# Projecting queries and keys of two batches at once, routing in six steps, and moved weight preparation in a two-layer decoder with routed experts

## The chip, the cores and the metric

The kernel runs on one core of one Trainium2 chip. The metric is the device time of one execution in microseconds (us). Three runs of the kernel before took 1874.07, 1877.6 and 1878.22 us, so the median is 1877.6 us. All data is 32-bit float.

The core has a matrix engine (TensorE, PE in the profile, with its weight loads as PEld), a vector engine (DVE), an activation engine (ACT), a general engine (GpSimd, POOL) and a queue that issues transfers (SyncE, SP). Each engine works through its own instructions in the order of the program. Matrix results go to PSUM, which this kernel divides into 4 banks for scores and a ring of 4 more for everything else.

## The reference, cut to what matters

There are 32 batches (B) of 100 rows (S) with 256 features (D), and a context of 361 rows (SK) per batch. Attention has 16 heads of 16 features. Two post-norm decoder layers follow each other:

```python
x = layernorm(x + self_attention_0(x))              # has its own inner residual; q, k, v with bias
x = layernorm(x + cross_attention_0(x, ctx, dist))  # adds -log(dist) to the scores
x = layernorm(x + ffn_0(x))        # layernorm, clip(xn * 128 / gamma), weights rounded to -1, 0, 1
x = layernorm(x + self_attention_1(x))              # one 16x16 q, k, v weight for all heads
x = layernorm(x + cross_attention_1(x, ctx))
x = layernorm(x + moe(x))          # logits = x @ Wg + bg; the best of 8 experts, weighted by its probability
```

`gamma` is the largest absolute value of `xn` over all batches, so layer 1 can begin only when the attention of layer 0 has ended for all of them. The rounding of the feed-forward weights needs `beta`, the mean absolute weight. The last step sends each row through one expert with two 256x256 layers.

## The kernel before, in words

**Slots.** The attention of both layers is written as a list of slots. `plan_batch` (L343 to L489) puts closures at a slot number and a place from 0 to 3, and `run_slots` emits them in that order; there is no planner that weighs costs. A batch begins at `start = LAYER[l] + 5 * b`, and its self-attention at `early`, which for all but the first four batches is 18 slots ahead of it. Per slot, `run_slots` emits the scores of the step two slots ahead, the transposes and exponentials of the next step, and the sums of the present one:

```python
ahead, nxt, now = (steps.get(s + d) for d in (2, 1, 0))
centre = ahead.scores() if ahead else []
for do in centre[:2]:
    do()
side(0)
for do in centre[2:]:
    do()
for i in range(3):
    if nxt:
        nxt.turn(i)
    side(i + 1)
if now:
    now.sums()
```

A batch has one self step (16 heads at once) and four cross steps of four heads each, so five slots hold one self and four cross steps, each of another batch.

**A cross step.** PE computes scores (`sc_x`, L225). DVE adds the bias and finds the maximum in one custom instruction per head (L308), POOL subtracts the maximum (L312), PE transposes the result (L322), ACT takes the exponential (L323), PE sums over the context with the values (L332), ACT copies the sums (L334). A self step does maximum and subtraction of all heads on DVE (L266, L269), then transposes (L279), exponential (L280), sums (L286). The four score banks have one buffer: the scores of a slot wait until DVE has read those of the slot before.

**Around the steps.** Rows are transposed to features by PE with a copy on ACT (`transpose_rows`, L194 and L197). `project` makes queries or keys of one batch: four matmuls with 100 columns, each of which shows as two records, in one bank (L207); layer 1's self weight is a 128x128 diagonal block and needs two matmuls (L204). `mask_queries` scales the queries for heads of even and odd number (DVE L217, or ACT L215 where there is no bias). Keys of the context (L420, L422) and values (L433, copies L436 and L439) take two and three chunks per batch; the first two value chunks share a bank. The sums are turned and normalised (L235, L237, L239), transposed again, and multiplied by the output weight (L251); DVE adds the residual (L252), takes statistics (L73, L75), POOL turns the variance into a scale (L77, L78), and DVE writes the rows back to `x_all` (L82).

**Layer 0's end.** The feed-forward input `xn` (L444, L445) and its maximum (L446) are made per batch. `scale_of_all` reduces the maximum over partitions on POOL (L642). Layer 1 then clips `xn` (L373, L374), multiplies by the rounded weights (L380) and adds the residual (L382) ahead of its self-attention.

**Weights.** `round_weights` (L632 to L638, slot 14 place 3) takes the sum of absolute weights on DVE, reduces it over partitions on POOL (L633), and makes the rounded weights on DVE. `fold_value_bias("l1x")` (L163, L166, L167, slot 18) and `fold_heads` (L651, L655, slot 22) prepare layer 1's weights: PE matmuls whose result goes into a bias row or over the weights.

**Routing.** `router` (L454, L455) makes the logits of a batch at `start + 10`, place 1. At the last batch of a group of four (batches 28 to 30 are a group of three, 31 is alone), `probabilities` (`start + 10`, place 3: 12 DVE instructions around one exponential on ACT) and `places` (`start + 11`, place 3) follow: DVE counts the rows of the batches before (`ahead`, L553 and L554, two instructions a batch), PE adds them up (`r_p`, L557: one matmul that reads `hot`, one that reads `ahead`), DVE makes the row numbers (L559 to L561). `send` (`start + 12` on) scatters the rows to their expert's region. When all are sent, `block_table` and the expert stage follow.

## Time and profile before

| | us |
|---|---|
| median of three runs | 1877.6 |
| profiled execution | 1869.26 |
| its span, which the profile shows | 1867.5 |
| PE busy in it | 1745.7 |
| stretch 420 to 680, layer 0 in steady state: PE busy | 260.00 of 260 |
| stretch 880 to 990, the passage between the layers: PE busy | 93.43 of 110 |
| stretch 1124 to 1229.7, four batches of layer 1: PE busy | 102.09 of 105.7 |
| stretch 1760 to 1867, mostly the experts: PE busy | 72.40 of 107 |

The profile comes from one execution, 8.3 us below the median of the runs shown. Its times are counted from the start of the span. "Busy" is the time in which an engine had an instruction in work; matmuls overlap in the pipeline, so the last of a group shows a longer duration than it costs. The granted clock is the clock of PE, where 1.00 is full speed. The chain that ended last is followed back from the last instruction to what released it, so its lines give what a group cost on the path. A wait is put down to the instruction that ended last before it.

### The profile page before, as it was taken

The page shows a single profiled execution, that of the slowest core. Times are in us where ns is not written, and L with a number is a line of the kernel's source. Part 1 is how long each engine was busy: PE and PEld are TensorE (multiplying, and loading weights), DVE is VectorE, ACT ScalarE, POOL GpSimd, SP SyncE. Part 2 cuts the span into 40 slices and gives each one's busy share as a digit, 9 for nine tenths or more (in the row PEclk, how much of TensorE's full clock was granted, in tenths as well). Part 3 has the DMA queues.
Part 4 walks back from the last instruction along what each step waited for, and adds up shares of the span by engine and source line. Part 5 has one row for each costly group of instructions (what it writes and reads, how often), then busy time and mean ns, then how long its engine had stood idle before and what let it go on. Part 6 is the DMA issues. An engine that isn't in the chain of part 4 may idle for free.

```text
span 1867.5 us, 53553 instructions
## 1 busy us (share of the span) xinstructions
PE 1745.7 (93%) x21368; PEld 1334.3 (71%) x21368; DVE 1313.3 (70%) x3973; ACT 918.1 (49%) x2285; POOL 1115.9 (60%) x1687
## 2 busy tenths in 40 slices
PE   6998999999999999998799999999999999999595
PEld 5776777777777777765567777777777777776484
DVE  4665667767677676777687777777777777766576
ACT  2553555555555555554345545454545545454242
POOL 1464566666666665665166576666657666655467
PEclk9998999999999999999999999999999999999798
DMA  3200222222222322200000000000000000000094
GB/s 98 65 24 20 59 64 77 79 79 60 63 76 79 79 61 62 72 27 18 17 2 18 18 27 10 27 18 22 16 16 27 18 27 10 27 18 18 32 364 160
DMA packets 62038, 95.75 MB, mean 51 GB/s; under 512 B 7675, under 2 KB 45821, under 8 KB 61662
## 3 DMA queue, kind: packets, MB, share of 16 engines
q1 hardware_dynamic: 56190, 84.68, 15.3%
q0 software_dynamic: 3584, 6.59, 1.1%
q8 instruction: 169, 2.77, 0.6%
q10 hardware_dynamic: 2016, 1.06, 0.2%
q14 instruction: 79, 0.65, 0.1%
HBM read 58.38 MB, written 34.84 MB: 50 GB/s over the span
## 4 chain that ended last, share of the span: by engine, by line
PE 83%; DVE 8%; POOL 3%; issue 3%; ACT 1%; DMA 1%; SPq 0%; POOLq 0%; DVEq 0%; ACTq 0%
PE r_t_x L322 14%; PE sc_x L225 11%; PE r_v L433 9%; PE r_a_x L332 8%; PE r_k L420 7%; PE r_q L207 5%; PE r_t_s L279 4%; PE r_o_x L251 3%; PE sc_s L225 3%; PE r_o_s L251 3%; PE r_a_s L286 3%; PE r_n_s L235 2%; PE r_k L207 2%; DVE pr L308 2%; POOL out_dram L565 2%
## 5 line engine op out<-in xcount | busy, mean ns | idle before, releaser
L312 POOL TENSOR_TENSOR pr<-pr,mx_x 100x361 f32<-100x361 f32 x992 | 761.1, 796 | 517.0 <-DVE mx_x L308 508.3
L323 ACT ACTIVATE pT_x<-r_t_x 120x400 f32<-120x400 f32 (+1 forms) x768 | 373.8, 504 | 317.9 <-PE r_t_x L322 310.8
L322 PEld LDWEIGHTS r_t_x<-ident,pr 100*120 100x120 f32 (+1 forms) x3072 | 318.1, 140 | 111.5 <-issue 45.5
L322 PE MATMUL r_t_x<-ident,pr 100*120 100x100 f32 (+1 forms) x3072 | 386.2, 253 | 9.8 <-POOL pr L312 9.4
L308 DVE CUSTOM_DVE_ANT_0 pr<-sc_x,dist 100x361 f32<-100x361 f32 x512 | 246.5, 530 | 144.9 <-PE sc_x L225 132.2
L308 DVE CUSTOM_DVE_ANT_0 pr<-sc_x,zero 100x361 f32<-100x361 f32 x512 | 244.3, 529 | 132.5 <-PE sc_x L225 129.9
L225 PE MATMUL sc_x<-kT_x,qz_x 32*100 32x361 f32 x2048 | 224.4, 508 | 10.4 <-DVE pr_s L269 8.1
L332 PE MATMUL r_a_x<-pT_x,v_cross 120*32 120x100 f32 (+1 forms) x6144 | 186.5, 254 | 8.0 <-ACT kT_x L422 8.0
L332 PEld LDWEIGHTS r_a_x<-pT_x,v_cross 120*32 120x32 f32 (+1 forms) x6144 | 129.6, 110 | 40.9 <-ACT kT_x L422 13.0
L280 ACT ACTIVATE pT_s<-r_t_s 100x400 f32<-100x400 f32 x256 | 121.2, 503 | 67.7 <-PE r_t_s L279 67.4
L266 DVE TENSOR_REDUCE mx_s<-sc_s 100x16 f32<-100x1600 f32 x64 | 116.5, 1820 | 37.3 <-PE sc_s L225 37.3
L279 PE MATMUL r_t_s<-ident,pr_s 100*100 100x100 f32 x1024 | 120.4, 250 | 5.1 <-DVE pr_s L269 2.3
L269 DVE TENSOR_TENSOR pr_s<-sc_s,mx_s 100x1600 f32<-100x1600 f32 x64 | 116.8, 1824 | 2.2
L279 PEld LDWEIGHTS r_t_s<-ident,pr_s 100*100 100x100 f32 x1024 | 100.5, 130 | 20.0 <-issue 7.8
L225 PEld LDWEIGHTS sc_x<-kT_x,qz_x 32*100 32x100 f32 x2048 | 68.7, 161 | 51.3 <-issue 20.1
L433 PE MATMUL r_v<-c_l1x_wv,ctx 128*120 128x256 f32 (+1 forms) x384 | 102.0, 390 | 0.0
L433 PE MATMUL r_v<-c_l0x_wv,ctx 128*120 128x256 f32 (+1 forms) x384 | 100.4, 384 | 0.0
L334 ACT COPY avs_x<-r_a_x 128x100 f32<-128x100 f32 x256 | 61.4, 240 | 59.9 <-PE r_a_x L332 52.1
L420 PE MATMUL r_k<-ctx,c_l1x_wk 128*128 128x361 f32 x256 | 90.3, 476 | 0.0
L420 PE MATMUL r_k<-ctx,c_l0x_wk 128*128 128x361 f32 x256 | 90.1, 474 | 0.0
L217 DVE SCALAR_TENSOR_TENSOR qz_x<-r_q,qm_x_scale,qm_x_bias 128x200 f32<-128x200 f32 x128 | 48.4, 419 | 54.0 <-PE r_q L207 52.1
L308 DVE DVE_READ_ACCUMULATOR2_ANT mx_x<- 100x1 f32 x1024 | 84.0, 82 | 0.0
(217 smaller groups left out, 2947.4 us busy)
## 6 DMA issues: line engine op xcount, KB each, us to landing
regions<-no_token SPq DMA_DIRECT2D x23, 1161.0 KB
ctx<-in_ctxT_dram SPq DMA_DIRECT2D x64, 361.0 KB
wb<-in_experts_dram SPq DMA_DIRECT2D x32, 513.0 KB
dist<-in_dist_dram SPq DMA_DIRECT2D x32, 141.0 KB
xb<-regions SPq DMA_DIRECT2D x32, 129.0 KB
x_all<-in_x_dram SPq DMA_DIRECT2D x32, 100.0 KB
b<-in_b_dram SPq DMA_DIRECT2D x1, 1024.0 KB
regions<-x_all,place POOLq DMA_INDIRECT x32, 2.9
```

The source lines that it names most:

```text
L207: nc.tensor.matmul(ps[:, m, :], lhsT=w[:, k, m * P:(m + 1) * P], rhs=srcT[:, k, :], start=(k == 0), stop=(k == NC2 - 1))
L225: nc.tensor.matmul(dst, lhsT=qz[rows, p, k, :], rhs=kT[rows, k, :], start=True, stop=True)
L269: nc.vector.tensor_tensor(pr, sg, mx.unsqueeze(3).to_broadcast([S, NG, NG, S]), ALU.subtract)
L279: nc.tensor.transpose(pt[:, j, :], t["pr_s"][:, j, g, :], ident[:S, :S])
L280: nc.scalar.activation(t["pT_s"][:, g], pt, AF.Exp)
L308: nc.vector.tensor_tensor_reduce(pr[:, j, :SK], sc[:, j, :], bias, 1.0, LOWEST, ALU.add, ALU.max, mx)
L312: nc.gpsimd.tensor_tensor(pr[:, j, :SK], pr[:, j, :SK], mx.to_broadcast([S, SK]), ALU.subtract)
L322: nc.tensor.transpose(pt[:n, j, :], t["pr_x", g][:, j, k0:k0 + n], ident[:S, :S])
L323: nc.scalar.activation(t["pT_x", g][:n, i], pt[:n], AF.Exp)
L332: nc.tensor.matmul(av[32 * j:32 * j + 32, :], lhsT=t["v_x"][:n, i, head(g, j), :], rhs=t["pT_x", g][:n, i, j, :], start=(i == 0), stop=(i ...
L420: nc.tensor.matmul(ps, lhsT=c[sx + "_wk"][:, k, m * P:(m + 1) * P], rhs=t["ctx"][:, k, :], start=(k == 0), stop=(k == NC2 - 1))
L433: nc.tensor.matmul(ps, lhsT=t["ctx"][:, k, k0:k0 + n], rhs=c[sx + "_wv"][:, k, :], start=(k == 0), stop=(k == NC2 - 1))
```

## The change

- `plan_pair` is new. It takes the transposes, queries and keys of self-attention, the cross queries and the feed-forward of layer 0's end out of `plan_batch` and plans them for two batches at a time. `project` now has 200 columns per matmul, `mask_queries` 400 elements, the clip 400. The tiles of a pair have one buffer (`w1`), but for the masked cross queries, which have two.
- For the first four batches `early` is two slots sooner; a pair's cross queries are made nine slots ahead of its first batch (four ahead for the first pair) instead of four slots ahead of each.
- Each value chunk has a bank and a copy of its own, and the chunks stand in slots `kv + 2`, `kv + 3` and `kv + 4`.
- The router moves one slot later. `probabilities` and `places` are cut into six steps, from `start + 11`, place 3, on, alternating between places 3 and 1. The rows are sent three slots later.
- The rounding is cut: mean at slot 14, rounding at slot 18. The two folds move to slot `SLOTS * B + 3`, in the passage between the layers. Layer 1 begins three slots later.

In the program order of the changed kernel, PE has 288 matmuls fewer, DVE 96 masks and 32 clips fewer, ACT 32 key copies and 32 masks fewer and 64 value copies more; POOL has the same instructions. In the odd batches of layer 1 the first feed-forward of a pair stands in the slot of the self scores, ahead of the normalising of the cross sums on DVE. In the slot of `ahead` and `r_p` the next pair's rows are turned and its self queries projected. `L167` of the fold stands on DVE between the statistics of the last batch and the writing of its rows.

```diff
-LAYER = (0, SLOTS * B + 20)
+LAYER = (0, SLOTS * B + 23)
...
-        def project(ps, w, srcT):
+        def project(w, srcT, tag):
+            ps = bank(tag)[:, :NC2 * 2 * S].rearrange("p (m b s) -> p m b s", m=NC2, b=2)
...
-                    nc.tensor.matmul(ps[:, m, :], lhsT=w[:, k, m * P:(m + 1) * P], rhs=srcT[:, k, :],
+                    nc.tensor.matmul(ps[:, m], lhsT=w[:, k, m * P:(m + 1) * P], rhs=srcT[:, k],
                                      start=(k == 0), stop=(k == NC2 - 1))
...
+        def plan_pair(l, b):
+            first = starts(l, b)
...
+            def turned(key, kind, i):
+                if i == 0:
+                    u[key] = w1.tile([P, NC2, 2, S], F32, tag=f"xT_{kind}", name=f"xT_{kind}{tag}")
+                transpose_rows(xs[b + i], kind, f"{l}_{b + i}", dst=u[key][:, :, i, :])
...
+            early = first[1]
...
+            if l:
+                at(early - 8, 2, clipped)
+                for i in range(2):
+                    at(early - 7 + i, 1, lambda i=i: feed_forward(i))
+                    at(early - 6 + i, 1, lambda i=i: centre_and_scale(xs[b + i], both[i]["y_f"], both[i]["ln_f"]))
+            for i in range(2):
+                at(early - 4, 0, lambda i=i: turned("xT", "s", i))
+            at(early - 4, 2, self_queries)
+            if l == 0:
+                at(early - 3, 1, self_keys)
+            cross = first[0] - (9 if b else 4)
+            for i in range(2):
+                at(cross, 0, lambda i=i: turned("x2T", "x", i))
+            at(cross, 2, cross_queries)
+
+        def starts(l, b):
+            return LAYER[l] + SLOTS * b, LAYER[l] + (2 * b - 10 if b < 4 else SLOTS * (b - 4) + 2)
...
-                at(early - 7, 2, keep("xq", clipped))
-                at(early - 6, 1, keep("ln_f", feed_forward))
-                at(early - 5, 1, lambda: centre_and_scale(xs[b], t["y_f"], t["ln_f"]))
-            at(early - 4, 0, keep("xT", lambda: transpose_rows(xs[b], "s", tag)))
-            at(early - 3, 0, self_queries)
-            if l == 0:
-                at(early - 3, 1, self_keys)
...
-            at(start - 4, 0, keep("x2T", lambda: transpose_rows(xs[b], "x", tag)))
-            at(start - 4, 2, keep("qz_x", cross_queries))
...
-            at(kv + 2, 3, lambda: cross_values(1))
-            at(kv + 3, 1, lambda: cross_values(2))
+            at(kv + 3, 1, lambda: cross_values(1))
+            at(kv + 4, 1, lambda: cross_values(2))
...
-                at(start + 10, 1, router)
+                at(start + 11, 1, router)
...
-                    at(start + 10, 3, lambda: probabilities(first, n))
-                    at(start + 11, 3, lambda: places(first, n))
+                    for i, do in enumerate((centred_logits, exponentials, one_hot, ahead_of, counted, rows_of)):
+                        at(start + 11 + (i + 1) // 2, 3 if i % 2 == 0 else 1, lambda do=do: do(first, n))
...
-        at(14, 3, round_weights)
-        at(18, 3, lambda: fold_value_bias("l1x"))
-        at(22, 3, fold_heads)
+        at(14, 3, mean_weight)
+        at(18, 3, rounded_weights)
+        at(SLOTS * B + 3, 0, lambda: fold_value_bias("l1x"))
+        at(SLOTS * B + 3, 0, fold_heads)
```

## The prediction, made before the changed kernel ran

> **What bounds the kernel now.** I read the page first: the busy shares, the slices with the granted clock, the chain that ended last, by engine.

> ```profile
> span 1867.5 us, 53553 instructions
> PE 1745.7 (93%) x21368; PEld 1334.3 (71%) x21368; DVE 1313.3 (70%) x3973; ACT 918.1 (49%) x2285; POOL 1115.9 (60%) x1687
> PE 83%; DVE 8%; POOL 3%; issue 3%; ACT 1%; DMA 1%; SPq 0%; POOLq 0%; DVEq 0%; ACTq 0%
> ```

> TensorE (PE) carries the end; the DVE and POOL shares say where something else does. The busy time by stretch shows where that is (us, then busy us of PE, PEld, DVE, ACT, POOL, granted clock, DMA).

> ```profile
> 150.30:158.00 7.70, 0.00 (x0) 0.00 (x0) 5.30 (x8) 0.24 (x1) 0.40 (x1) 0.68 0.00 0
> 420.00:680.00 260.00, 260.00 (x3309) 200.46 (x3308) 186.75 (x551) 142.70 (x352) 164.00 (x242) 1.00 0.27 71
> 897.00:912.00 15.00, 9.92 (x69) 7.31 (x67) 7.04 (x14) 3.73 (x10) 1.65 (x4) 0.89 0.09 25
> 1043.60:1068.80 25.20, 24.89 (x323) 18.92 (x322) 18.54 (x56) 13.32 (x34) 15.80 (x25) 1.00 0.05 17
> 1068.80:1098.80 30.00, 27.30 (x328) 20.70 (x327) 21.58 (x77) 13.37 (x35) 17.92 (x28) 0.94 0.07 21
> 1077.60:1079.80 2.20, 0.05 (x2) 0.01 (x1) 1.96 (x11) 0.46 (x1) 1.60 (x4) 1.00 0.00 0
> 1079.80:1085.50 5.70, 5.70 (x50) 4.25 (x51) 3.84 (x16) 1.25 (x3) 3.10 (x5) 0.70 0.00 0
> ```

> Layer 0 in steady state is pure PE. Layer 1 is nearly so, except that one batch in four takes 30.0 us. The waits name what PE waits for there (total us, times, longest); the third line is the rounding (8.0 us), seen from the weight loads.

> ```profile
> PE r_p L557 <- DVE ahead L553: 20.3, 10, 2.7
> PE r_a_x L332 <- ACT kT_x L422: 8.0, 26, 0.3
> PEld sc_x L225 <- DVE pr_s L269: 12.6, 27, 8.0
> ```

> Last, the chain in order of time gives what a group costs PE from its start to the next (start, us, group), free of the pipeline's tail.

> ```profile
> 1022.89 1.24 PE r_k L420 x4
> 1025.34 0.89 PE r_q L207 x8
> 1029.73 0.88 PE r_v L433 x4
> 1048.14 1.24 PE r_k L420 x4
> 1103.34 1.24 PE r_k L420 x4
> ```

> The plan has five slots to a batch; slot 0 starts with the self scores (sc_s), slots 1 to 4 with cross scores (sc_x). Times below are us.

> **Projecting two batches at once.** A record of 100 columns costs PE 0.89/8 = 0.111 us, of 256 columns 0.220, of 361 columns 0.310. No row has 200 columns. It costs no more than 256 (0.220); from the slope between 256 and 361 (0.857 ns a column) 0.172, which I take, as 0.310/361 and 0.220/256 both give 0.86 ns a column. A pair of projections falls from 16 x 0.111 = 1.78 to 8 x 0.172 = 1.38: 0.40 saved (by the upper end 0.02). Layer 0 has three per pair of batches, layer 1 one and a half (its self weight has half the records): 16 x 4.5 x 0.40 = **29 us of PE** (upper end: 1.5). Whether PE's time is the end's time goes by slot.

> Layer 0: three projections make 0.60 per batch, and the 0.08 by which the r_q at 413.61 waited on ACT makes 0.68. Against it stands slot 0: sc_s at 418.12, the two self passes on DVE (1.82 each) end at 423.33, sc_x follows at 423.38. It cannot shrink, and the xn work (L444 to L446, 1.4) that precedes those passes on DVE now follows r_o_s in a slot 4 where it has less time: the passes start 1.65 after sc_s instead of 1.54. I charge 0.1. So 0.58 x 28 steady batches = 16, and 1 for the four without a self step, where PE waits for POOL's pr: **-17** (0 at the upper end of 200 columns).

> Layer 1: the slots, from one scoring group of the chain to the next (1015.83, 1020.92, 1027.24, 1032.67, 1036.95, 1041.07), take 5.1, 6.3, 5.4, 4.3 and 4.1. I move PE's groups between them.
> - Slot 0 loses the router matmul (0.30) and a wait of 0.47 that it causes by holding a PSUM bank until DVE has read it (r_a_x for kT_x, 25 times), but DVE's two passes hold the slot at 4.9. On odd batches r_f (0.86) comes in instead and the wait stays: 5.7.
> - Slot 1 gains the router. Even: one transpose more (0.17), the pair's q for one (+0.49), no r_f: 6.4. Odd: no transpose, no q (0.89): 5.6. There y_f and its statistics (1.15) now come ahead of rc_x and o_x on DVE: pr_s ends 4.65 after sc_s, o_x so 6.5 to 6.6, and r_x_ox, which PE reaches at 6.45, waits up to 0.2: 5.8.
> - Slot 2 gives one value chunk (0.88) to slot 4, which loses r_q (0.45): 4.55 both.
> - Slot 3 loses or gains a transpose, and on odd batches gains q (4 x 0.172): 4.1 and 5.1.

> Even 24.5, odd 25.7, against 25.25: 0.16 x 28 = **-4.5** (0 with a longer wait for o_x; -15 if DVE holds no slot).

> DVE's masks are one 128x400 for two 128x200 (420 each; by the slope of 100x256 to 100x1600, 1.04 ns an element, 627): 20 us less DVE work. One PSUM bank and one copy per value chunk adds 0.16 of ACT per batch, hidden at 13.3 busy of 25.2; a full bank ring would cost the 0.47 of the row above.

> **Routing in six steps.** Per group of four the chain grows by 1103.34 - 1048.14 - 2 x 25.25 = 4.7: 2.2 waiting for `ahead`, about 2 at clock 0.70, 0.3 for r_p itself. Six groups cost 4.7 and one 3.1: 31. After: the eight `ahead` operations (1.6 in the trace) stand half a slot before the matmul, in slot 3 behind four centrings, rc_s and o_s. Before, DVE's last centring in slot 3 ended 3.5 after sc_x (1036.1 against 1032.6), so `ahead` ends at about 5.0; PE reached the same place 3.4 after sc_x (1036.0) and now has 0.17 + 0.69 more ahead of it: 4.3, and 0.1 for the first half of r_p. Left are a wait of 0.5 and 0.3 of matmul: 7 x 0.8 = 5.5, **-25.5**. Behind ahead, x_all (0.7) waits on DVE; r_x_m needs it a slot later.

> [...]

> **Rounding split.** Now DVE waits 5.4 for the all-reduce, so pr_s and PE stop for 7.7 and the clock (0.53 to 0.68) costs 2.5. DVE is freed, but POOL is not: all-reduce and the reload behind it hold it from 147.1 to 159.35, then y_x, y_s and four centrings (3.0) come. PE runs on to the first r_t_x that needs them (sc_x at 150.9, a slot of 5.6, 0.8 of scores: 157.3) and gets through it at 163.8 instead of about 157.7: a wait of 6, and 2.5 for the clock behind it as now, 8.6 to 9; the five rounding operations (1.8) put 1 on a self slot later. Against 10.2 now I take **0** (-4 if the clock holds, +1).

> **Folds moved.** Their slots go: the slot with fold_l1x ran from sc_x at 171.60 to 178.47, 6.87 instead of 4.29, and the batch with fold_heads (r_k 186.72 to 213.89) 27.17 instead of 25.92: **-3.8**. In the passage r_fold_l1x stands behind r_k (4 x 0.6 at half clock) and DVE's add (L167) waits for it ahead of the last x_all, on the chain to the maximum: +2.1.

> **Passage.** LAYER[1] is 3 slots later, at no cost by itself: empty slots issue nothing. POOL's reload (rs_f at 902.65, 12.7 after gmax) hides the doubled clip. Then two rs_f, two transposes and a pair's q come before sc_s: +1.5, mostly covered by r_f on DVE. Later the first sc_x stands behind r_o_s, r_a_s, r_n_s of the last self batches, which used to run beside its centring: +2 to +3, less 1.5 of work done ahead. With the fold **+4** (0 to +7). **Start**: q and k of a pair at half clock put the first sc_s 2 later, half regained: +1. **Tail**: r_o_x of the last batch no longer waits 3.4 for routing, but its x_all does: -1.

> **Sum**: -17 - 4.5 - 25.5 + 0 - 3.8 + 4 + 1 - 1 = -46.8. The profiled execution took 1869.3 (span 1867.5 and 1.8 around it), so 1822.5; the median of the runs is 1877.6, 8.3 above, so **1831**. Own range 1822 to 1840.

> **Rivals.**
> - *PE's time counts in full* (0.2): slot 0 and y_f bind nowhere, r_p meets no wait. 29 + 31 + 3.8 + 2 - 3 = 63: 1815. For it: 260.00 of 260.00 busy. Against: pr_s and sc_x are 0.05 apart.
> - *A new wait for the removed one* (0.15): DVE runs later than counted, r_p waits 2 again and the clock falls, odd batches lose what even ones gain. Routing 10, layer 1 0: 1877.6 - 27 = 1851.
> - *The slow clock is not the wait's* (0.05): routing gains 12.6 less: 1843. Against: twice 0.70 right behind such a wait.
> - *Slower* (0.05): cross queries of a pair are now turned in slot 1, and the second batch's x_all is written by DVE at the end of slot 0: it ended at 424.27, PE asks near 424.5. If DVE is late there by 2.2, as at r_p, each of 32 pairs pays 4.7: 150, so 1981. It decides from 46.8/32 = 1.5 us a pair. Against: DVE has about 3 us of rest in the slots before.
> - *The split does nothing* is in the sum.

> **Chances.** Forecast 0.55, rivals 0.45. The range goes to the full gain with rounding's better end, 1808, and to the new wait, 1851; outside are the slower case and the tails. A measurement here tells 0.2% (3.8 us) from no change. Faster 0.93, same 0.02, slower 0.05.

> **What would show it.** PE has 576 records fewer, r_q of 128x200 at 0.17. Layer 0's period 25.3 for 25.92; layer 1's pair 50.2 for 50.5; group batches without 30 us. r_p <- ahead under 1 us each. Around the rounding PE idles for r_t_x <- pr, not for pr_s. I am wrong if 200 columns cost over 0.2, if r_x_ox <- o_x or r_x_x <- x_all appears with over 1 us, or if PE's clock falls anywhere in the steady state.

## The result, and the profile after

The changed kernel took 1858.78 us (median of 4 runs, 1857.05 to 1860.14) where the kernel before took 1876.65 (median of 4, 1874.07 to 1878.22): a ratio of 0.9906 with a 95% interval of 0.9888 to 0.9923. It is faster by 0.9%, as far as the sign goes, but the forecast was 1831 with a range of 1808 to 1851, and the time lies outside it. The profiled execution has a span of 1858.2 against 1867.5: 9.3 us less, where the sum of the prediction had 46.8 less.

From the page of the changed kernel: the span, the busy time of the engines, and the chain that ended last, by engine.

```profile
span 1858.2 us, 52208 instructions
PE 1734.3 (93%) x20792; PEld 1317.6 (71%) x20792; DVE 1296.3 (70%) x3845; ACT 913.3 (49%) x2285; POOL 1115.2 (60%) x1687
PE 80%; DVE 9%; POOL 5%; issue 3%; DMA 1%; ACT 1%; SPq 0%; POOLq 0%; DVEq 0%; ACTq 0%
```

The 576 records fewer are there, yet PE's busy time fell by 11.4 us only, and POOL has 5% of the chain instead of 3%. A shorter program that is hardly shorter in time has new waits or a lower clock somewhere. To find the place, I cut the span at one event that occurs in every batch, the first record of r_x_ox, and compare the lengths of the stretches, in us:

| stretch | before | after | difference | forecast |
|---|---|---|---|---|
| start to the first batch of layer 0 | 99.3 | 105.6 | +6.3 | +1 |
| layer 0, first to last batch | 782.8 | 759.5 | -23.3 | -17 - 3.8 + 0 = -20.8 |
| passage: last of layer 0 to first of layer 1 | 89.0 | 104.1 | +15.1 | +4 |
| layer 1, first to last batch | 780.9 | 774.1 | -6.8 | -4.5 - 25.5 = -30.0 |
| last batch to the end | 115.5 | 114.9 | -0.6 | -1 |
| sum | 1867.5 | 1858.2 | -9.3 | -46.8 |

So two stretches hold the miss: layer 1 (23 us) and the passage (11), with 5 at the start. Within layer 1 the batches tell which step it is. Those that follow each other without a group take 24.78 and 25.33 (50.1 the pair; 50.49 before, 50.2 forecast). There are seven full groups; six are routed in this steady part, the seventh in the layer's last batches, which have no self steps beside them. A batch in which one of the six is routed takes 28.9 to 29.0 (one of them 27.35) and the next 26.2 to 26.7, so that a group still costs 4.2 + 0.9 to 1.4, against 4.7 before: nothing of the 25.5 us came.

The busy time by stretch of the changed kernel (us; then busy us and instructions of PE, PEld, DVE, ACT, POOL; granted clock, DMA). The first line is the wait at the rounding, the second a stretch of layer 0 (a little over ten batches), the third the passage, the fourth and fifth the two slots around r_p of one group.

```profile
161.42:166.57 5.15, 0.01 (x2) 0.00 (x1) 0.02 (x1) 0.55 (x2) 2.11 (x4) 0.81 0.00 0
414.54:674.51 259.97, 259.86 (x3273) 198.84 (x3269) 189.53 (x539) 143.59 (x357) 164.77 (x245) 1.00 0.31 77
865.12:969.21 104.09, 86.47 (x874) 64.06 (x874) 63.62 (x146) 36.62 (x91) 34.84 (x60) 0.86 0.03 8
1078.44:1086.38 7.94, 5.88 (x70) 4.60 (x66) 6.68 (x28) 4.20 (x10) 4.01 (x7) 0.99 0.01 2
1086.38:1092.43 6.05, 6.05 (x58) 4.26 (x54) 3.24 (x13) 2.42 (x6) 3.03 (x4) 0.73 0.19 50
```

Read the last two against the same slots of another batch, 5.30 and 4.56. The first is 2.64 longer: PE is idle for 2.06 of it, and r_p takes the rest. The second is pure PE (6.05 of 6.05) and still 1.49 longer: its clock was 0.73. This is the picture of before, a wait and a slow slot behind it, moved by one slot. The waits of PE say the same (total us, times, longest):

```profile
PE r_p L585 <- DVE ahead L579: 19.2, 9, 3.5
PE r_t_x L326 <- POOL pr L316: 12.3, 20, 5.1
```

Before, r_p waited 20.3 us in 10 times. Why it still waits is seen on the engines in order of time. PE (start, us, group; what the idle time before it ended):

```profile
1082.82 0.28 PE L585 MATMUL r_p<-hot,c_below 100*100 100x32 f32 x2
1085.16 0.36 PE L585 MATMUL r_p<-ahead,ones 100*100 100x32 f32 x2 [2.06 <-DVE ahead L579]
```

and DVE and POOL in the same slot, whose scores PE began at 1078.44:

```profile
1080.19 0.19 DVE L573 TENSOR_TENSOR hot<-hot,col 100x32 f32<-100x32 f32 x1
1080.31 0.54 DVE L312 CUSTOM_DVE_ANT_0 pr<-sc_x,zero 100x361 f32<-100x361 f32 x1
...
1082.75 0.59 DVE L579 COPY ahead<-sofar 100x8 f32<-100x8 f32 x1
1083.38 0.71 DVE L580 TENSOR_TENSOR sofar<-sofar,hot 100x8 f32<-100x8 f32 x1
1084.12 0.17 DVE L579 COPY ahead<-sofar 100x8 f32<-100x8 f32 x1
```

```profile
1080.93 3.13 POOL L316 TENSOR_TENSOR pr<-pr,mx_x 100x361 f32<-100x361 f32 x4 [1.47 <-DVE mx_x L312]
```

PE reached r_p 4.4 us after the slot's scores, as forecast. But the eight operations of `ahead` ended 6.9 after them, not 5.0 (the last copy, for which r_p waits, at 6.7). One part is `one_hot`: its eight operations (1.7 us) stand half a slot earlier, so DVE began to centre only at 1080.31, 1.9 after the scores began, and its last centring ended 4.4 after them instead of 3.5. (In the same slot of a batch without routing it ends 3.6 after them, in the changed kernel as in the one before.) The other part is `ahead` itself: its first two operations, of 8 elements, took 0.59 and 0.71 us instead of 0.17, until POOL's centring ended at 1084.06, and all eight 2.56 instead of 1.6. It is the same in all six groups. In the kernel before, POOL's centring was all but over when `ahead` began (it ends at 1078.44):

```profile
1075.41 3.03 POOL L312 TENSOR_TENSOR pr<-pr,mx_x 100x361 f32<-100x361 f32 x4 [6.45 <-DVE mx_x L308]
1078.33 0.16 DVE L553 COPY ahead<-sofar 100x8 f32<-100x8 f32 x1
```

5.0 + 0.9 + 1.0 is 6.9.

### The profile page after: what moved, and what is told of

It reads as the page before. It is cut to its first block, busy times and chain, and to the rows that moved or that the text cites. A ratio compares the mean times of both kernels' runs of the same rounds, so it can differ in the third digit from the quotient of the medians.

```text
span 1858.2 us, 52208 instructions
## 1 busy us (share of the span) xinstructions
PE 1734.3 (93%) x20792; PEld 1317.6 (71%) x20792; DVE 1296.3 (70%) x3845; ACT 913.3 (49%) x2285; POOL 1115.2 (60%) x1687
## 3 DMA queue, kind: packets, MB, share of 16 engines
q1 hardware_dynamic: 56190, 84.68, 16.2%
## 4 chain that ended last, share of the span: by engine, by line
PE 80%; DVE 9%; POOL 5%; issue 3%; DMA 1%; ACT 1%; SPq 0%; POOLq 0%; DVEq 0%; ACTq 0%
PE r_t_x L326 13%; PE sc_x L229 11%; PE r_v L471 8%; PE r_a_x L336 8%; PE r_k L460 7%; PE r_t_s L283 5%; PE r_o_x L255 3%; PE sc_s L229 3%; PE r_a_s L290 3%; PE r_o_s L255 3%; PE r_qx L209 2%; POOL pr L316 2%; DVE pr L312 2%; DVE pr_s L273 2%; DVE mx_s L270 2%
## 5 line engine op out<-in xcount | busy, mean ns | idle before, releaser
L327 ACT ACTIVATE pT_x<-r_t_x 120x400 f32<-120x400 f32 (+1 forms) x768 | 379.2, 503 | 313.5 <-PE r_t_x L326 309.9
L326 PEld LDWEIGHTS r_t_x<-ident,pr 100*120 100x120 f32 (+1 forms) x3072 | 324.1, 139 | 140.4 <-issue 44.5
L326 PE MATMUL r_t_x<-ident,pr 100*120 100x100 f32 (+1 forms) x3072 | 397.3, 254 | 13.5 <-POOL pr L316 12.3
L270 DVE TENSOR_REDUCE mx_s<-sc_s 100x16 f32<-100x1600 f32 x64 | 116.4, 1819 | 31.8 <-PE sc_s L229 31.0
L473 ACT COPY v_cross<-r_v 120x256 f32<-120x256 f32 (+1 forms) x192 | 71.5, 372 | 85.1 <-PE r_v L471 85.1
L471 PE MATMUL r_v<-c_l1x_wv,ctx 128*120 128x256 f32 (+1 forms) x384 | 107.3, 404 | 0.0
L220 DVE SCALAR_TENSOR_TENSOR qz_x<-r_qx,qm_x_scale,qm_x_bias 128x400 f32<-128x400 f32 x64 | 37.6, 630 | 70.9 <-PE r_qx L209 70.8
```

Source lines behind the costliest of these rows:

```text
L270: nc.vector.tensor_reduce(mx, sg, AX.X, ALU.max)
L326: nc.tensor.transpose(pt[:n, j, :], t["pr_x", g][:, j, k0:k0 + n], ident[:S, :S])
L327: nc.scalar.activation(t["pT_x", g][:n, i], pt[:n], AF.Exp)
L471: nc.tensor.matmul(ps, lhsT=t["ctx"][:, k, k0:k0 + n], rhs=c[sx + "_wv"][:, k, :], start=(k == 0), stop=(k == NC2 - 1))
```

## The experiments

Each kernel is compared with the kernel before in the same series of runs; medians of that kernel were 1870.5 to 1876.7 from series to series, so that small differences are read between kernels of one series, or from the stretches. The first two series take the routing apart.

**r_p half a slot later**, in the changed kernel, with the rows behind it:

```
-   at(start + 11 + (i + 1) // 2, 3 if i % 2 == 0 else 1, lambda do=do: do(first, n))
+   at(start + 11 + (i + 1 + (i > 3)) // 2, 3 if (i + (i > 3)) % 2 == 0 else 1, lambda do=do: do(first, n))
```

> The changed kernel with the routing matmul (r_p) and the rows behind it half a slot later; nothing else moves. Wait theory: a group costs because PE reaches r_p 2.06 us before DVE's ahead is done, and 3.4 us at half clock follow; the slots of 7.95 and 6.05 go back to about 5.6 and 4.6 (5.30 and 4.56 in other batches, 0.3 for r_p), so 3.8 x 7 = 27 less: 1832 us. Rival, the clock falls there whatever PE waits for: only the wait goes, 2.06 x 7 = 14: 1844. Rival, it is the routing work of DVE and POOL that fills the slots: 1858, no change.

Measured: 1844.18 (ratio 0.9838, 0.9821 to 0.9855), not 1832. It is the number of the first rival, but not its mechanism: the clock does not fall in any of the six full groups of the steady part (it does at the seventh). The line of the slot after the one with `ahead`, and what PE waits for in it:

```profile
1082.72:1088.84 6.12, 4.95 (x63) 3.70 (x59) 4.34 (x18) 2.95 (x9) 3.36 (x5) 1.00 0.19 57
```

```profile
1084.75 0.36 PE L194 MATMUL r_x_m<-ident,x_all 100*128 100x100 f32 x2 [1.17 <-DVE x_all L82]
```

r_p no longer waits for `ahead`, but the residual's x_all stands behind `ahead` on DVE, and the transposes that need it wait 1.17. The group's batch took 26.35 (28.97 in the changed kernel), of which 1.6 stayed. A wait of 1.2 leaves the clock at 1.00 where one of 2.06 was followed by a fall: the slow slots were the wait's.

**The third and fourth send of a group three slots later.** Each send has a conversion and an indirect DMA on POOL (1.0 to 1.3 us):

```
-   at(start + 15 + i, 1, lambda i=i: send(first + i))
+   at(start + 15 + (i if i < 2 or b > B - 4 else i + 3), 1, lambda i=i: send(first + i))
```

> The changed kernel with the third and fourth send of a group three slots later, in slots in which POOL has rest. Theory: the 0.3 and 0.6 us that the slots of 4.88 and 6.20 have over 4.56 and 5.63 come from POOL, which issues an indirect DMA (1.0 to 1.3 us) ahead of the four centrings there; 0.9 x 6 groups = 5.4 less, 1853.5 us. Rival, those slots are long for another reason (DVE's clip on double time): 1858.8, within 1.5.

Measured: 1860.01, but its runs lie between 1842 and 1868, so the median decides nothing. The trace does: the batch behind a group takes 25.33 instead of 26.2 to 26.7, as in any other place (slots of 4.55 and 5.63). So the sends cost 0.9 to 1.4 a group, some 5 us in all, because they were moved from slots in which POOL had rest to those in which it doesn't. How they cost it is seen on DVE: with the sends ahead of it, POOL's centring is late and runs beside the two clips (L382, L383) that DVE makes ahead of the self step's maximum, and the clips take twice as long. First the changed kernel, then this one, where POOL's centring ended at 1114.63:

```profile
1115.45 3.27 POOL L316 TENSOR_TENSOR pr<-pr,mx_x 100x361 f32<-100x361 f32 x4
1117.34 0.75 DVE L382 TENSOR_SCALAR xq<-xnT,xscale 128x400 f32<-128x400 f32 x1
1118.12 0.83 DVE L383 TENSOR_SCALAR xq<-xq 128x400 f32<-128x400 f32 x1
```

```profile
1114.62 0.40 DVE L382 TENSOR_SCALAR xq<-xnT,xscale 128x400 f32<-128x400 f32 x1
1115.05 0.37 DVE L383 TENSOR_SCALAR xq<-xq 128x400 f32<-128x400 f32 x1
```

So the maximum begins 1.7 us after the self scores instead of 1.0, which is the 0.6 of that slot. The rival named the clips, and they are the way; but the sends are what makes them long. The 0.3 of the slot before was not followed up.

**Routing undone**: router, two steps and sends as in the kernel before, the rest as changed:

```
-   at(start + 11, 1, router)
+   at(start + 10, 1, router)
-   at(start + 11 + (i + 1) // 2, 3 if i % 2 == 0 else 1, lambda do=do: do(first, n))
+   at(start + 10 + i // 3, 3, lambda do=do: do(first, n))
```

> The changed kernel with the routing in two steps, the router and the sends three slots earlier, as in the kernel before; all else stays changed. Wait theory: r_p waits about 2.2 us and the clock halves for 3.4 us in both, so a group costs 4.7 instead of 4.1 + 0.9: 1857 us, within 3. Rival, the six steps do gain what they were forecast to gain (25 us), and something else took it back: 1880 or more.

Measured: 1871.33 (ratio 0.9982, 0.997 to 0.9994), between the two. PE waited 25.5 us for `ahead` (19.2 with six steps), and group batches took 30.3 to 32.0. So my expectation was off: in the new order of slots two steps are worse than they were in the old one, and the change's routing (six steps, later sends) is worth some 13 us against them. Compared with the kernel before, they only pay for the new order.

**The kernel before with nothing but r_p moved** half a slot later (and the sends by a slot):

```
-   ps = bank(f"p_{first}")[:S, :n * E]
+   routed["ahead"] = ahead
+
+def counted(first, n):
+   hot, ahead = routed["hot"], routed["ahead"]
+   ps = bank(f"p_{first}")[:S, :n * E]
...
+   at(start + 12, 1, lambda: counted(first, n))
```

> The kernel before with nothing but r_p and the rows behind it half a slot later (the sends one slot later). Wait theory: the wait of 2.2 us and the half clock behind it go, 30.0 us become 25.6: 4.3 x 7 = 30 less, 1847 us. Rival, only the wait goes and the clock stays: 2.2 x 7 = 15, 1861. Rival, the work of routing on DVE is the price: 1876, no change.

Measured: 1848.98 (ratio 0.9868, 0.9851 to 0.9884): 24.5 us from one moved matmul, more than the whole change. The group's batch of 30.0 became 26.4, no full group has a fall of the clock (1.00 from 1071 to 1102, around the first of them), and the runs agree within 1.1 us (1848.66 to 1849.78), where those of the kernel before lie 10 us apart, with a mean granted clock of 0.974 to 0.980. So whether the clock falls behind such a wait seems to differ from run to run.

The second series begins here. **All steps of a group spread over eight slots**, in the changed kernel: `one_hot` behind the residual's x_all in a slot where DVE has rest (4.38 us busy of 5.30 with it there), `ahead` three slots later, r_p a slot behind it, the sends in slots 20, 21, 25 and 26. (The last two groups keep the changed order.)

```
+   calm = b < B - 4
+   when = ((11, 3), (12, 1), (13, 2), (16, 2), (17, 2), (19, 3)) if calm else \
+       ((11, 3), (12, 1), (12, 3), (13, 1), (13, 3), (14, 1))
...
+       at(start + ((20, 21, 25, 26)[i] if calm else 15 + i), 1, lambda i=i: send(first + i))
```

> The changed kernel with the six steps of every full group spread over eight slots instead of three: DVE's one_hot behind the residual's centring in the slot that has most rest, ahead three slots later, r_p a slot behind ahead, and the sends in slots 20, 21, 25 and 26. With r_p half a slot later alone the clock stayed at 1 and 2.6 us of a group's 4.1 went; 1.2 us stayed as a wait for x_all, which stands behind ahead on DVE, and 0.9 behind the sends. Theory (the wait only moved along DVE's queue): with the steps apart, group batches take 24.8 + 0.3 and the batches behind them 25.3, so 1844 - (1.3 + 0.9) x 6.5 = 1830 us, and the runs lie within 3 us of each other. Rival, DVE's routing work costs its time wherever it stands: 1844.

Measured: 1830.12 (ratio 0.9764, 0.9747 to 0.978), runs within 4.3 us. The group's batch takes 24.78, not a hundredth more than one without, and the batch behind it 26.18, still 0.85 more than in any other place, where 25.3 was expected; what that is was not taken apart. The 25 us of the forecast exist; the change's own order did not collect them.

The other three of this series have the same routing, so that differences of some us can be seen.

**Folds behind the maximum**: scale_of_all is cut behind POOL's all-reduce, and the folds stand in the gap.

```
-   at(SLOTS * B + 3, 0, lambda: fold_value_bias("l1x"))
-   at(SLOTS * B + 3, 0, fold_heads)
    at(SLOTS * B + 4, 3, scale_of_all)
+   at(SLOTS * B + 4, 3, lambda: fold_value_bias("l1x"))
+   at(SLOTS * B + 4, 3, fold_heads)
+   at(SLOTS * B + 4, 3, scales)
```

> The same with the three weight folds of layer 1 issued behind the maximum of all batches, while POOL reduces it, instead of ahead of it. Theory: DVE's add to the bias waits 2.3 us for r_fold_l1x on the chain to the maximum; gmax comes 2.6 us earlier behind the last r_x_ox and all behind it too: 2.6 us under the kernel with the routing spread alone. Rival, POOL's 12 us between the maximum and its next instruction cover it: 0.

Measured: 1828.42 (0.975, 0.9733 to 0.9766) beside 1830.12: no difference that these runs can tell. gmax came 0.8 us earlier behind the last r_x_ox, but the passage was 105.6 us long instead of 104.1.

**A shorter lead of the first self steps**, as before, with the first pair's cross queries last in the slot ahead of its scores:

```
-   LAYER[l] + (2 * b - 10 if b < 4 else SLOTS * (b - 4) + 2)
+   LAYER[l] + (2 * b - 8 if b < 4 else SLOTS * (b - 4) + 2)
-   cross = first[0] - (9 if b else 4)
+   cross, place = (first[0] - 9, 0) if b else (first[0] - 3, 3)
```

> Routing spread, and the first four self steps of each layer two slots closer to the cross steps (the lead of the kernel before), with the cross queries of the first pair formed last in the slot ahead of its scores. Theory: the longer lead makes each layer's first cross scores wait for the chain of the last self steps, 15.5 us behind the last self scores instead of 10.5 at the start, and 15.9 instead of 8.6 in the passage; some of it stays, as the second batch's x_all must come first: 4 us less in each layer, 8 under the kernel with the routing spread alone. Rival, the pair's queries need all of that lead: within 2 us of it.

Measured: 1828.35 (0.9761, 0.9741 to 0.978), from 1822.6 to 1832.1. Its trace has a passage of 97.9 us with a granted clock of 0.93, 6.2 shorter, and the start is unchanged; the median tells no more than 2. Inconclusive by itself; why, is seen below.

**The sum of magnitudes on PE** instead of POOL's all-reduce:

```
-   nc.gpsimd.partition_all_reduce(beta, asum, P, bass_isa.ReduceOp.add)
+   nc.gpsimd.memset(everyone, 1.0)
...
+   nc.tensor.matmul(ps, lhsT=everyone, rhs=asum, start=True, stop=True)
+   nc.vector.tensor_scalar(beta, ps, 1.0 / (D * D), None, ALU.mult)
```

> Routing spread, and the sum of the weights' magnitudes over partitions by one matmul with ones instead of POOL's all-reduce (a memset on POOL stays). Theory: at the rounding PE waits for POOL, which the all-reduce and what follows it hold for 12 us; without it the batch of 36.1 us falls to 27: 9 us under the kernel with the routing spread alone, and no half clock there. Rival, it is DVE's rounding of the weights that holds the slot: 2 less at most.

Measured: 1823.04 (0.9724, 0.9708 to 0.974), 7.1 less. In the changed kernel the rounding's slot began at 160.56 and POOL did this (start, us; idle time before):

```profile
157.32 0.40 POOL L665 PARTITION_ALL_REDUCE beta<-asum  x1 [5.59 <-DVE x_all L82]
164.46 0.71 POOL L248 TENSOR_TENSOR y_x<-x_all,c_l0x_bo 100x256 f32<-100x256 f32 x1 [6.73 <-issue]
```

Without the all-reduce the same slot has no wait and no fall of the clock:

```profile
160.88:165.43 4.55, 4.55 (x65) 3.34 (x61) 2.85 (x11) 3.22 (x8) 2.91 (x5) 1.00 0.10 33
```

In layer 0, 9.4 us are gone by the trace; some of it comes back in the passage (107.5 us, clock 0.84).

The third series starts from **three cures at once**, the spread routing, the shorter lead and the sum on PE.

> The changed kernel with three of the cures at once: routing spread over eight slots, the shorter lead of the first self steps, the sum of magnitudes by a matmul. Theory (they act at different places, so their gains add): 1830.1 less 7.1 for the sum and less 4 for the lead, 1819 us, within 3. Rival, the lead's gain in the trace (6.2 us in the passage) was chance, as its runs lay 10 us apart: 1823.

Measured: 1822.21 (0.9735, 0.972 to 0.9751). The rival's number: the lead adds nothing to 1823.04 that these runs can tell. Here the passage took 107.8 us at a clock of 0.84.

**The three cures and the folds behind the maximum**:

> The same with the folds of layer 1 behind the maximum. Theory: 2.3 us of DVE's wait leave the chain to the maximum, 2 us less than without that. Rival, what follows is set by POOL and by which stretches get half the clock, as in the one trace so far (gmax 0.8 earlier, first cross score 3 later): 0, within 1.5.

Measured: 1821.24 (0.973, 0.9714 to 0.9746), the rival again, although this trace's passage is 101.5.

**The three cures, projections one batch at a time**: the same banks, masks and order, but for each block of weights two matmuls of 100 columns:

```
-   nc.tensor.matmul(ps[:, m], lhsT=w[:, k, m * P:(m + 1) * P], rhs=srcT[:, k], ...)
+   for i in range(2):
+       for k in range(NC2):
+           nc.tensor.matmul(ps[:, m, i], lhsT=w[:, k, m * P:(m + 1) * P], rhs=srcT[:, k, i], ...)
```

> The three cures, but every projection of a pair as two of 100 columns for each block of weights (16 records of 100 columns a pair and weight instead of 8 of 200); all else as in the kernel with the cures. Theory: a pair's projections cost PE 0.40 more each, 72 of them, 29 us of PE, and the slot in layer 0 that DVE holds takes some of it up: 20 in layer 0 and 5 in layer 1, 25 us more. Rival, DVE holds more slots now that PE is faster: 12 more. Rival, 200 columns cost as much as 256 (0.220): 1.5 more.

Measured: 1847.89 (0.9882, 0.9867 to 0.9897), 25.7 more. The sum is the theory's 25, its parts are not: layer 0 is 16.2 and layer 1 9.5 us longer, where 20 and 5 were expected. A pair and the group behind it with 200 columns:

```profile
421.79 1.54 PE L209 MATMUL r_q<-xT_s,c_l0s_wq 128*128 128x200 f32 x8
423.17 0.51 PE L326 MATMUL r_t_x<-ident,pr 100*122 100x100 f32 x4
```

and with 100:

```profile
431.51 1.95 PE L211 MATMUL r_q<-xT_s,c_l0s_wq 128*128 128x100 f32 x16
433.30 0.51 PE L328 MATMUL r_t_x<-ident,pr 100*122 100x100 f32 x4
```

From start to start 1.38 and 1.79: 0.172 us for a record of 200 columns, and 0.41 a pair.

**The three cures, the first pair's cross queries alone**: in each layer batch 0 and 1 are turned and projected in the places of the kernel before.

```
+   if b == 0:
+       for i, slot in enumerate((first[0] - 4, first[0] - 1)):
+           at(slot, 0, lambda i=i: turned("x2T", "x", i))
+           at(slot, 2, lambda i=i: query_alone(i))
+       return
```

> The three cures, and the cross queries of each layer's first two batches formed one by one in the places of the kernel before; the other pairs stay pairs. Theory: what is left of the passage's loss (97.9 us from the last r_x_ox of layer 0 to the first of layer 1 with the shorter lead, 89.0 in the kernel before) is the first pair's queries waiting for the second batch's x_all: 6 of the 8.9 go, and 2 at the start, 8 less than the three cures alone. Rival, it is the self queries and POOL's power of two batches ahead of the first self scores: 2 less at most.

Measured: 1812.58 (0.9687, 0.9673 to 0.9702), 9.6 less than the three cures, and all runs (1809.8 to 1816.5) lie below all of theirs (1817.5 to 1823.5).

The last series asks whether the first pair is the passage's whole loss. **The first pair's self queries and keys alone as well**:

```
+   for i in range(2 if b == 0 else 0):
+       at(early - 4 + 2 * i, 0, lambda i=i: turned("xT", "s", i))
+       at(early - 4 + 2 * i, 2, lambda i=i: self_query_alone(i))
+       if l == 0:
+           at(early - 3 + 2 * i, 1, lambda i=i: self_key_alone(i))
```

> The three cures, the first pair's cross queries one by one, and now also its self queries and keys one by one, in both layers: nothing of the first two batches is formed as a pair but the clip. Theory: in the passage the first self scores stood 8.1 us behind POOL's first power (4.1 in the kernel before), as the pair's queries wait for the second batch's x_all; 4 of that go in the passage and 1 at the start, and the stretch at half clock (26.8 us, 10.2 before) becomes shorter: 5 to 9 less than with the cross queries alone, 1805. Rival, the passage's length is set by the clock's stretches, which fall as they may: 1812, within 2, with runs as far apart as before.

Measured: 1808.52 (0.964, 0.9622 to 0.9658), between the two numbers, with runs now within 2.3 us and a passage of 94.8 (100.1 with the cross queries alone). The kernel before was 4.7 slower in this series; by the ratios (0.964 and 0.9687) the step is worth 8.8 us, inside the theory's 5 to 9. **And the folds behind the maximum**:

> The same with the folds of layer 1 behind the maximum. Theory: DVE's wait of 2.3 us for a fold leaves the chain to the maximum: 2 less. Rival: within 1, as in the two pairs of kernels so far (1.7 and 1.0 less, each inside the spread).

Measured: 1808.07 (0.9637, 0.9619 to 0.9655): the third pair of kernels in which the folds' place is not to be told from nothing. This is the fastest kernel here, 3.6% under the kernel before. **The changed kernel, with the shorter lead and its first pairs alone and no other cure**:

> The changed kernel itself (its routing, its all-reduce and its folds kept) with the shorter lead and with the first two batches of each layer formed one by one. Theory: the passage goes from 104.1 to about 91 and its stretch at half clock from 29.9 to 10 us or so, the start gives 3: 1858.8 - 15 = 1844, with the 8 us of spread that the waits of routing bring. Rival, the first pair is not what makes the passage long (folds on the chain, a longer queue on POOL): 1855.

Measured: 1846.6 (0.9847, 0.9826 to 0.9868), 12.2 less than the changed kernel's median, or 11 by the ratios. Its start is 100.0 (105.6) and its passage 95.6 (104.1). The passage of the kernel before, and of this one, beside the 104.09 at 0.86 above:

```profile
882.14:971.15 89.01, 74.58 (x868) 54.83 (x868) 61.12 (x145) 36.04 (x91) 33.78 (x58) 0.94 0.04 10
```

```profile
859.87:955.50 95.63, 81.23 (x887) 60.22 (x887) 63.36 (x148) 37.06 (x93) 34.86 (x60) 0.91 0.03 9
```

PE's idle time is 14.4 us before, 17.6 after and 14.4 here; the rest of the difference is PE busy longer with nearly the same instructions: 74.6, 86.5, 81.2. Two things make it so. What the clock withheld is 0.06 x 89.0 = 5.3 us before, 0.14 x 104.1 = 14.6 after, 0.09 x 95.6 = 8.6 here; counted only while PE was busy, 5.1, 13.4 and 7.8. And the folds' matmuls, which the change put here, take PE 2.35 us (r_fold_l1x begins at 870.33 and the r_k behind it at 872.68). So of the 15.1 us, by this estimate, 8 to 9 are the clock, 2.4 the folds, 3.2 idle time. The traces that disagreed go the same way: one kernel with the shorter lead had a clock of 0.93 and 97.9 us, another 0.84 and 107.8.

## Why the prediction was wrong, point by point

- **Projecting two batches at once: right.** The record of 200 columns costs 0.172, the mask of 128x400 0.630 (0.627 forecast), and undoing it costs 25.7 us where PE's share was put at 29. Layer 0 has 24.68 and 26.09 for its two batches, 25.39 on average (25.3 forecast). That its whole sum came so near (-23.3 for -20.8) is in part luck: 22 steady batches gave 11.8 (0.58 each would be 12.8), but the last five, most of them without a self step, gave 6.0 where some 1.5 was put. In layer 1 the slots by hand were 24.5 and 25.7, and came out at 24.46 and 25.66.
- **Routing in six steps: wrong, and the largest part of the miss.** The step that failed is "so `ahead` ends at about 5.0". The 3.5 us to DVE's last centring came from a batch in which `one_hot` did not stand ahead of it (0.9), and the 1.6 us of `ahead` from a place in which POOL wasn't centring (1.0). With 6.9 for 5.0, the wait was 2.06 instead of 0.5, and the clock fell behind it as before. The rival that said this ("r_p waits 2 again and the clock falls") had a chance of 0.15, and even it left a gain of 10 that was not there: I didn't count where the sends went, three slots on, at 0.9 to 1.4 a group. The sign that was named for being wrong, a fall of the clock in the steady state, is there five times.
- **The clock: as taken.** The forecast put about 2 us of a group's price down to a slow slot behind the wait, and gave 0.05 to the rival that the slow slot is not the wait's. No run shows the 12.6 us of that rival (an estimate, 1.8 for each of seven groups): the slow slot cost 1.49 (6.05 against 4.56), and it went with the wait. The kernels without that wait in the six full groups (r_p half a slot later in either kernel, the spread routing with and without more) have no fall of the clock there: 1.00 from 1077.41 to 1088.84 in the changed kernel with r_p later, from 1071 to 1102 in the one before with r_p later, from 1076.84 to 1086.70 with the routing spread. A wait of 2.05 to 2.06 us was followed by a fall in five groups of six, one of 1.17 by none.
- **Rounding split: right.** PE waits 5.14 at r_t_x for POOL's pr (6 forecast), and the slots around it are 10.1 longer than usual, where they were 10.4 before. With the sum on PE they are 0.5 longer: it was POOL's to hold. What the prediction calls POOL's reload shows in the traces only as idle time behind the all-reduce, put down to "issue" (6.86 us before, 6.73 after).
- **Folds moved: right, but half told.** Batches with a fold are no longer longer in layer 0. In the passage they delay gmax by up to 2.6 us (2.1 forecast); that their 2.35 us of PE go there too I didn't count. To issue them behind the maximum shows nothing in three pairs of kernels, as it leaves their work in the passage.
- **Passage and start: right in sign, wrong in size.** +4 became +15.1, and +1 became +6.3 (some 1 of it a later first load). I charged the first sc_x behind the last self steps with 2 to 3 us; in the passage it came 15.9 behind the last sc_s instead of 8.6. Not counted was the clock: 29.9 us of the passage ran at 0.50, 10.2 before, which is 8 to 9 us by the estimate above. With the first pair taken apart (and the shorter lead) 8.5 us of the passage and 5.7 of the start are back; of the latter up to 2 are chance, as kernels with the same start show 103.5 to 105.9. The other 6.6 of the passage are, by the trace, about 3 of clock and 2.4 of folds; about 1 stays open.
- **Tail: not to be told.** -0.6 for -1, but kernels that end like the changed one show tails from 114.0 to 115.9.
- **The base.** The forecast for the profiled execution was put 8.3 higher to compare with the median. The one after (1860.1) lies 1.4 above its median, so the medians differ by 17.9 where the profiles differ by 9.1. The kernel before scatters by 10 us; as the kernel with r_p moved scatters by 1, that seems to come from its group waits, and its one profile was a short one.

## What to carry to other kernels

When an instruction is moved to get ahead of a consumer, lay out the queue of its engine in the new slot with everything that moves along with it, and take each duration from a place with the same neighbours; here 0.9 and 1.0 us decided 25. If a wait is worth removing, move the consumer rather than the producer: one matmul half a slot later did more than six steps. And a change that pays in steady state by pairing things has its price at each fill of the pipeline, where nothing covers the wait for the second one; leave the first pair single.

## What was not expected of the hardware

```profile
1502.60:1506.02 3.42, 2.30 (x18) 2.02 (x16) 3.32 (x13) 2.69 (x6) 3.07 (x4) 1.00 0.02 5
1506.02:1509.43 3.41, 2.48 (x42) 1.68 (x43) 1.51 (x8) 0.67 (x3) 0.00 (x0) 1.00 0.00 0
1608.41:1611.83 3.42, 1.37 (x35) 0.98 (x33) 2.47 (x9) 1.55 (x4) 1.14 (x2) 1.00 0.00 0
1611.83:1615.24 3.41, 3.41 (x21) 2.16 (x18) 1.73 (x7) 1.07 (x3) 1.11 (x2) 0.50 0.00 0
```

Four traces (before, changed, sends moved, changed with the first pairs alone) have 24 such waits of 2.05 to 2.15 us. Of 16 with at least 1.47 of idle time in one window 15 were followed by a fall, of five with at most 1.32 none, and of three in between two. Of the 12 in the first two of these traces, nine had 1.47 to 2.15, and a fall followed each; of 1.37 and 1.38 the first was followed by one, and 1.12 was not.

Two small DVE operations took longer beside POOL's centring. The copy of `sofar` (8 elements a partition) and the sum behind it took 0.59 and 0.71 us while POOL's centring ran and 0.17 right behind it; the centring passes of DVE itself stayed at 0.53. The last two of POOL's four instructions of 0.79 end at 1083.32 and 1084.06, the two DVE operations at 1083.34 and 1084.08, and the third, behind them, is short. So each ended within 0.03 us of one of POOL's, in this group as in the other five, where they took 0.59 and 0.71 as well; what holds them the trace doesn't name. The two clips (128x400), 0.75 and 0.83 beside POOL's centring and 0.40 and 0.37 without it, go the same way.
